# Two units' sums at once, a head in thirds, and four smaller moves in a hybrid scan, attention and STU kernel

## The chip, the cores and the metric

The kernel runs on one core of one Trainium2 chip. A core has a matrix engine (PE, with PEld for its weight loads), a vector engine (DVE), a scalar engine (ACT), GpSimd (POOL) and a queue that issues transfers (SP). Each works its own instructions in the order of the program; they meet through semaphores. The metric is the device time of one execution in microseconds (us), the median of several runs: 5449.74 us for the kernel before (three runs, 5448.53 to 5450.31).

## The reference

Four images of 48 x 48 positions and 128 channels, all in float32. Two layers follow each other:

```python
x = x + conv_ssm(gn(x))        # layer 0
t = tokens(x)                  # 2304 tokens of 128
t = t + attention(ln(t))       # softmax(q q^T) q, no projections
t = t + ffn(ln(t))             # spectral transform unit (STU)

# conv_ssm, cut: d = 256 inner channels, 16 states, K = 4 scan directions
xin, z = split(x @ in_proj)
xc = silu(depthwise_conv3x3(xin) + conv_b)
for each direction k:          # rows, columns, and both reversed
    dt = softplus(...);  B, C = projections of xc
    h = h * exp(dt * A) + dt * xc * B      # a recurrence over 2304 positions
    y_k = sum over the 16 states of h * C
y = layernorm(sum of y_k + D * xc) * silu(z) @ out_proj

# ffn, cut: 16 filters phi over the sequence, four sequence lengths mixed by weights
U_plus, U_minus = causal convolutions of u with each filter
out = sum_k U_plus @ M_plus[k] + U_minus @ M_minus[k] + three shifted products u @ M_u
```

## The kernel before

**Order of the work.** For each image b there is a prologue (norm, input projection, 3 x 3 convolution, silu), a scan pass, an epilogue with attention, and the STU. The prologue of image b + 1 runs inside the attention of image b, and the STU of image b inside the scan pass of image b + 1. So the program is: a head (prologue of image 0), pass 0, attention 0, pass 1 with STU 0, attention 1, pass 2 with STU 1, attention 2, pass 3 with STU 2, attention 3, and a last STU alone. The order is written out by hand with generators; the functions named below are all in one file.

**Head.** `prologue` makes a list of tasks. The convolution of one half of the channels (`taps`) is nine DVE operations over 128 x 2304 (L276, then L278 eight times); `silu` follows as a tanh on ACT (L287) and a product on DVE (L291) for each third of the half. `begin_scans` prepares the first chunks: projection xp (L412), dt (L429), softplus (L443), dx (L465), a store to DRAM and loads in the replicated form rep (L454, L459). It is a generator; in the head `begun` runs it through without anything between. `start_y` (L325) then starts the accumulators.

**Scan pass.** The 2304 positions in four directions are 24 chunks of 384. A chunk has eight units, (h, q): half of the channels, quarter of the states. A unit takes one step of the loop in `scans`: `enter` (L508, on DVE, or on POOL for three of the eight units) makes dt x B in a tile s, `decay` makes four decays on ACT (L517), `scan` runs four recurrences on DVE (L524), `times_c` multiplies by C (L534, POOL), and `sum_c` sums over the states by matmuls with a 128 x 32 matrix of ones (L542), four side by side on PE, into a y bank of the chunk. At step s the loop enters units s + 1 and s + 2, scans unit s, multiplies unit s - 1 and sums unit s - 2. There are six s tiles. The decays live in a `Ring` of PSUM banks (five in pass 0, four later), which also serves as space for the small products of `prep`; its constant zero columns are set once a pass (L341).

Between these, `more` takes the STU's work from a generator: it asks for the next piece while the columns done are fewer than the share of the pass that is over. `sum_c` adds its 384 columns to that count. The STU (`stu`) convolves with Toeplitz tables from DRAM: three products for each filter (L1192), copied by ACT between and after them (L1208, L1212, L1215, L1216), then projections (L1258). In pass 0 the generator is `mixture`, which mixes the weights.

**Attention.** Five pieces of up to 512 tokens, each in 18 slots. A slot is a score product (L852), an exp on ACT (L854) and, three slots later, a value product (L844). After a piece comes its `tail`, a generator that takes one step a slot: copy oT (L1043, DVE), transposes otr (L1047), denominators, the sum into T, a store td, and, for images that go on, a load tu, its statistics (L1072, then L1077 on POOL), the normed u (L1082, ACT), sums, transposes utr (L1088) and a store ud. The score products have three PSUM banks in turn.

**Last STU.** `stu3` works on three blocks of 128 rows by 16 filters. For each item it loads five tables (L1422) and a weight G (L1425), two items ahead; `begin` loads ux, mue and res for a block (L1431 to L1436). Five products (L1446) make x, y and i; DVE combines them into U (L1533 to L1537), and `project` multiplies by G (L1480) with U of the item before; the first time it also does the shifted products with mue (L1464). `finish3` prepares later blocks step by step beside it: a load fx (L1361), statistics (L1365), normed u (L1376).

What sets the order is thus the program order on each engine's queue. On SP all loads and stores stand in one line.

## Time and profile before

| | |
|---|---|
| median of three runs | 5449.74 us |
| profiled execution | 5450.86 us |
| its span, first to last instruction | 5448.9 us |
| PE busy | 4753.7 us (87%) |
| DVE busy | 4320.4 us (79%) |
| POOL busy | 3646.6 us (67%) |
| ACT busy | 3213.1 us (59%) |
| first to last scan of passes 0 to 3 | 117.8 to 1061.5, 1302.8 to 2258.4, 2497.5 to 3456.5, 3695.6 to 4651.1 |
| last STU, from its first product | 4847.0 |

The page gives busy times by engine, the span in 40 slices (a digit is tenths of busy time), the transfers, and groups of instructions by source line. Views of the trace used here are the timeline (start, length, engine, line, operation, and in brackets the idle time of that engine before it and what ended it), sums over windows, and lists of waits (who waited for whom: total, times, longest). PEclk is the granted share of PE's clock.

### The profile page before, as it was taken

To read this page: it belongs to the slowest core of one execution; us is meant where nothing else is said; L and a number is where in the kernel's file an instruction comes from. 1 tells how busy PE (TensorE), PEld (TensorE's weight loads), DVE (VectorE), ACT (ScalarE), POOL (GpSimd) and SP (SyncE) were. 2 spreads that over 40 slices of the span, in tenths; PEclk is the share of its full clock that TensorE was granted. 3 is DMA by queue.
4 is the path that set the end of the run, shared out by engine and by line. 5 is a ranking of instruction groups with operands and counts; after the bars stand their busy time and mean duration, and the time that the engine had idled before them with its cause. 6 is when DMAs were issued, how large, how long until landed. Compare 5 with 4: busy or idle time off the path is not lost. (4 is left out here: it accounts for less than half of the span.)

```text
span 5448.9 us, 71245 instructions
## 1 busy us (share of the span) xinstructions
PE 4753.7 (87%) x23372; PEld 3059.5 (56%) x23372; DVE 4320.4 (79%) x5308; ACT 3213.1 (59%) x6829; POOL 3646.6 (67%) x1881
## 2 busy tenths in 40 slices
PE   4656655698999999998999999898999999989999
PEld 1211211255666666645666666545666666559987
DVE  7999999856999999856999999658999999423211
ACT  3666666546777767456777766457777666432111
POOL 1999998713989999605999999407999999201100
PEclk7777777799999999999999999999999999999999
DMA  4445545404887777416777787227877786136543
GB/s 123 157 156 171 171 153 165 128 27 143 248 257 254 251 258 253 134 34 193 239 259 254 242 269 252 84 75 208 252 246 260 249 262 230 37 83 153 151 142 91
DMA packets 732184, 996.11 MB, mean 183 GB/s; under 512 B 108968, under 2 KB 580648, under 8 KB 731752
## 3 DMA queue, kind: packets, MB, share of 16 engines
q1 hardware_dynamic: 725992, 988.26, 57.6%
q10 hardware_dynamic: 5824, 3.30, 0.3%
q8 instruction: 187, 3.06, 0.2%
q14 instruction: 181, 1.48, 0.1%
HBM read 873.03 MB, written 118.31 MB: 182 GB/s over the span
## 5 line engine op out<-in xcount | busy, mean ns | idle before, releaser
L524 DVE TENSOR_TENSOR_SCAN s<-ring,s 128x385 f32<-128x385 f32 x3072 | 2691.5, 935 | 88.8 <-ACT ring L517 88.0
L534 POOL TENSOR_TENSOR s<-s,bc 128x1536 f32<-128x1536 f32 x763 | 2423.4, 3179 | 95.2 <-DVE s L524 39.0
L517 ACT ACTIVATE ring<-rep,A 128x384 f32<-128x384 f32 x3072 | 1760.2, 584 | 873.9 <-DVE s L508 537.2
L508 POOL TENSOR_TENSOR s<-rep,bc 128x1536 f32<-128x1536 f32 x288 | 994.7, 3454 | 152.4 <-DMA rep<-dtdud 81.2
L542 PE MATMUL y<-s,csum 128*32 128x384 f32 x6144 | 712.5, 538 | 184.0 <-POOL s L534 130.5
L508 DVE TENSOR_TENSOR s<-rep,ring 128x1536 f32<-128x1536 f32 x480 | 829.6, 1729 | 40.5 <-issue 19.9
L1192 PE MATMUL cx<-tt,u 128*128 128x252 f32 (+7 forms) x2880 | 621.9, 357 | 89.9 <-ACT cy L1208 88.9
L1192 PEld LDWEIGHTS cx<-tt,u 128*128 128x128 f32 x2880 | 501.7, 192 | 306.6 <-ACT cy L1208 135.4
L1192 PE MATMUL cx<-tt,us 128*128 128x252 f32 (+7 forms) x2880 | 617.3, 356 | 36.0 <-ACT U L1216 34.2
L1192 PEld LDWEIGHTS cx<-tt,us 128*128 128x128 f32 x2880 | 496.4, 193 | 196.7 <-issue 70.9
L1192 PE MATMUL cy<-tt,u 128*128 128x252 f32 (+5 forms) x2880 | 603.9, 351 | 0.0
L1192 PEld LDWEIGHTS cy<-tt,u 128*128 128x128 f32 x2880 | 490.7, 191 | 150.3 <-issue 99.4
L1258 PE MATMUL pr<-U,G 128*128 128x288 f32 (+4 forms) x1344 | 435.5, 451 | 6.8 <-DMA G<-gd 6.8
L1515 POOL TENSOR_TENSOR t<-s,s 128x512 f32<-128x512 f32 x48 | 63.4, 1320 | 521.7 <-ACT s L1513 521.7
L542 PEld LDWEIGHTS y<-s,csum 128*32 128x32 f32 x6144 | 126.0, 112 | 503.0 <-issue 237.8
L972 PE MATMUL G<-M,W 128*128 128x256 f32 (+3 forms) x512 | 242.3, 590 | 178.8 <-ACT Gm L948 81.2
L854 ACT ACTIVATE e<-s,shift 128x512 f32<-128x512 f32 (+1 forms) x360 | 230.7, 643 | 275.6 <-PE s L852 275.6
L852 PE MATMUL s<-xnT 128*128 128x512 f32 (+1 forms) x720 | 339.8, 557 | 12.9 <-ACT xnT L812 12.9
L844 PE MATMUL o<-e,xn 128*128 128x512 f32 (+1 forms) x720 | 335.4, 550 | 0.0
L1258 PEld LDWEIGHTS pr<-U,G 128*128 128x128 f32 x1344 | 232.4, 192 | 147.0 <-issue 89.2
L972 PEld LDWEIGHTS G<-M,W 128*128 128x128 f32 x512 | 106.9, 242 | 319.3 <-issue 111.3
L532 POOL COPY carry<-s 128x4 f32<-128x4 f32 x640 | 121.3, 189 | 230.8 <-DVE s L524 228.7
(236 smaller groups left out, 5029.5 us busy)
## 6 DMA issues: line engine op xcount, KB each, us to landing
rep<-dtdud SPq DMA_DIRECT2D x768, 384.0 KB
bc<-xdd SPq DMA_DIRECT2D x768, 192.0 KB
tt<-fd SPq DMA_DIRECT2D x144, 577.0 KB
tt<-fd SPq DMA_DIRECT2D x144, 451.0 KB
tt<-fd SPq DMA_DIRECT2D x144, 325.0 KB
dtdud<-dt SPq DMA_DIRECT2D x192, 192.0 KB
dtdud<-dx SPq DMA_DIRECT2D x192, 192.0 KB
t<-fd SPq DMA_DIRECT2D x80, 384.0 KB
```

The costliest lines, as they stand in the source:

```text
L508: eng.tensor_tensor(s, self.ch.rep[self.h][:, :, 1], bt.unsqueeze(1).to_broadcast([P, G4, CS]), ALU.mult)
L517: nc.scalar.activation(ring.body(self.dA[g]), ch.rep[self.h][:, g, 0], AF.Exp, scale=A[:, ch.k, self.h * G4 + g, self.q:self.q + 1])
L524: nc.vector.tensor_tensor_scan(s, ring.decays(i, ch.rev), s, 0.0, ALU.mult, ALU.add)
L532: nc.gpsimd.tensor_copy(carry[:, self.h, self.q].unsqueeze(2), self.s[:, :, end:end + 1])
L534: eng.tensor_tensor(self.s, self.s, ch.bc[Q4 + self.q].unsqueeze(1).to_broadcast([P, G4, CS]), ALU.mult)
L542: nc.tensor.matmul(ch.y[g * DL:(g + 1) * DL, :CS], csum, self.s[:, g], start=(self.q == 0), stop=(self.q == Q4 - 1))
L844: nc.tensor.matmul(po[J][:, :w], xn[:, i], e[:, :w], start=(i == 0), stop=(i == NT - 1))
L852: nc.tensor.matmul(p[:, :w], xnT[:, i * P:(i + 1) * P], xnT[:, 512 * J:512 * J + w], start=True, stop=True)
L854: nc.scalar.activation(e[:, :w], p[:, :w], AF.Exp, bias=shift)
L972: nc.tensor.matmul(p[:, :n], W[:, q if t else 0, i], M[t][:, i].unsqueeze(1).to_broadcast([P, n, C]), start=(t == 0 and i == 0), stop=(t = ...
L1192: nc.tensor.matmul(p4[:, 1:3, v - (hi - at):] if g else p4[:, 0:4:3, v - (hi - at):], x, t[:, :, hi - 1 - at + J * P:end if end >= 0 else ...
L1258: nc.tensor.matmul(o if q else o.rearrange("p f r m -> p r f m"), G, U[n][:, 4 * q:4 * q + 4, v0:v1].rearrange("p (a b) m -> p a b m", a=2 ...
```

## The change

Six places are edited.

1. **Head.** For image 0 the second half's convolution is done in thirds of 16 rows. The first third and its gate stay in the prologue; the operations of the other two thirds go into a list `late`, and the loop over `begin_scans` takes two of them after each of its first six pieces and one after each later piece. The prologue's pool moves to the other side of memory and is closed after that loop.
2. **Ring.** The zero columns are written by an ACT copy from the tile `none`, not by a DVE memset.
3. **STU ahead.** In passes 1 to 3 three steps of the STU are taken before the step loop begins.
4. **Sums.** `sum_c` is called at every second step, for units s - 3 and s - 2 together, and the count goes up by 768 there.
5. **Tail.** One more step between oT and otr; two more between the sums and utr.
6. **Last STU.** The five tables of the first item and the first mue are loaded in the last attention, 20 slots before its end, into a pool `pre` of their own; `fetch` leaves out the tables of item 0 and `begin` the first mue.

```diff
@@ -268,14 +268,14 @@
         def nothing():
             pass
 
-        def taps(h):
+        def taps(h, lo=0, hi=H):
             def tap(t):
                 dy, dx = divmod(t, 3)
-                x = xpad[:, dy:dy + H, dx:dx + W]
+                x, o = xpad[:, dy + lo:dy + hi, dx:dx + W], xc[h][:, lo:hi]
                 if t == 0:
-                    nc.vector.tensor_scalar(xc[h], x, cw[:, h, 0:1], cb[:, h:h + 1], ALU.mult, ALU.add)
+                    nc.vector.tensor_scalar(o, x, cw[:, h, 0:1], cb[:, h:h + 1], ALU.mult, ALU.add)
                 else:
-                    nc.vector.scalar_tensor_tensor(xc[h], x, cw[:, h, t:t + 1], xc[h], ALU.mult, ALU.add)
+                    nc.vector.scalar_tensor_tensor(o, x, cw[:, h, t:t + 1], o, ALU.mult, ALU.add)
             return [(nothing, Slow(lambda t=t: tap(t), 2.65), t == 0) for t in range(9)]
 
         def silu(h):
@@ -314,9 +314,18 @@
             if i % 2:
                 tasks.append(zs_[9 + i // 2])
                 tasks.append(silu(0)[i // 2])
-        tasks.extend(taps(1))
-        tasks.extend(silu(1))
+        if b:
+            tasks.extend(taps(1))
+            tasks.extend(silu(1))
+            return tasks
+        third, gates = H // 3, silu(1)
+        late[:] = [f for i in range(1, 3) for t in (*taps(1, i * third, (i + 1) * third), gates[i]) for f in t[:2]
+                   if f is not nothing]
+        tasks.extend(taps(1, 0, third))
+        tasks.append(gates[0])
         return tasks
+
+    late = []
 
     def start_y(b):
 
@@ -338,7 +347,7 @@
         def __init__(self, pool, n, name):
             self.t = [pool.tile([P, 512], F32, tag=f"ring{i}", name=f"{name}_{i}") for i in range(n)]
             for t in self.t:
-                nc.vector.memset(t[:, 0:CS + 2:CS + 1], 0.0)
+                nc.scalar.copy(t[:, 0:CS + 2:CS + 1], none[:, :2])
             self.free = list(range(n))
 
         def take(self):
@@ -666,6 +675,8 @@
         enter(-1)
         spread(1)
         fill(1)
+        for i in range(3 if units[0].ch.b else 0):
+            done[0] += next(work)
         for s in range(len(units) + 2):
             real = s < len(units)
             enter(s)
@@ -693,9 +704,10 @@
                 scan(s, 3)
             refill(s - 2, Q4)
             refill(s + 1, 0)
-            if s >= 2:
+            if s >= 2 and units[s - 2].q % 2:
+                units[s - 3].sum_c(back.psy)
                 units[s - 2].sum_c(back.psy)
-                done[0] += CS
+                done[0] += 2 * CS
                 if units[s - 2].q == Q4 - 1:
                     pending.append(units[s - 2])
             more((s + 1) / len(units))
@@ -1042,6 +1054,7 @@
         oT = pool.two.tile([P, 512], F32, tag="oT", name=f"oT{b}_{J}")
         nc.vector.tensor_copy(oT[:, :P * n], po[:, :P * n])
         yield
+        yield
         p = ps.trs.tile([P, 4, C], F32, tag="tr", name=f"otr{b}_{J}")[:, :n]
         for j in range(n):
             nc.tensor.transpose(p[:, j], oT[:, j * P:(j + 1) * P], ident)
@@ -1082,6 +1095,8 @@
             nc.scalar.activation(u[:k, J, j], x[:k, j], AF.Identity, bias=mv[:k, j, 3:4], scale=mv[:k, j, 2:3])
         yield
         nc.vector.tensor_tensor(sums[:k, J], u[:k, J, 0:2], u[:k, J, 2:4], ALU.add)
+        yield
+        yield
         yield
         p = ps.trs.tile([P, 512], F32, tag="tr", name=f"utr{b}_{J}")[:, :4 * k]
         for j in range(4):
@@ -1393,7 +1408,24 @@
             yield
         nc.sync.dma_start(ud3[:, :, 1 + P * G:1 + P * (G + 1)], x)
 
-    def stu3(b, pool, ps, u3, ue):
+    PT3 = (3, 1, 4, 0, 2)
+
+    def table3(pool, tag, k, pt, hi, name):
+
+        t = pool.tile([P, 2 * (L3 if tag == "tt" else P)], F32, tag=tag, name=name)[:, :2 * hi].rearrange(
+            "p (e i) -> p e i", e=2)
+        row = fd3[k, pt, 0]
+        nc.sync.dma_start(t, bass.AP(row.tensor, row.offset + L3 - hi, [[1, P], [L3 + P, 2], [1, hi]]))
+        return t
+
+    def mixed3(pool, bl):
+
+        parts = PARTS3[bl]
+        t = pool.tile([P, 3, 3, C], F32, tag="mue", name=f"mue3{bl}")
+        nc.sync.dma_start(t[:, :len(parts)], mud[:, parts[0][2]:parts[-1][2] + 1])
+        return t
+
+    def stu3(b, pool, ps, u3, ue, pre, ready):
 
 
 
@@ -1407,7 +1439,7 @@
         tts, Gs, S, U, now = {}, {}, {}, {}, {}
         last = pool.one.tile([P, KF], F32, tag="last", name="last3")
         nc.vector.memset(last, 0.0)
-        PT = (3, 1, 4, 0, 2)
+        tts.update({(0, pt): t for pt, t in zip(PT3, ready)})
         Y = 3 * (P + 1)
 
         def fetch(n):
@@ -1415,11 +1447,8 @@
                 return
             bl, k = items[n]
             hi = P * (bl + 1)
-            for pt in PT:
-                t = tts[n, pt] = pool.tt.tile([P, 2 * L3], F32, tag="tt", name=f"t3{n}_{pt}")[:, :2 * hi].rearrange(
-                    "p (e i) -> p e i", e=2)
-                row = fd3[k, pt, 0]
-                nc.sync.dma_start(t, bass.AP(row.tensor, row.offset + L3 - hi, [[1, P], [L3 + P, 2], [1, hi]]))
+            for pt in PT3 if n else ():
+                tts[n, pt] = table3(pool.tt, "tt", k, pt, hi, f"t3{n}_{pt}")
             parts = PARTS3[bl]
             Gs[n] = pool.tt3.tile([P, 2, 3, C], F32, tag="G", name=f"G3{n}")
             nc.sync.dma_start(Gs[n][:, :, :len(parts)], gd[k, :, :, parts[0][2]:parts[-1][2] + 1])
@@ -1430,8 +1459,7 @@
             now["x"] = pool.one.tile([P, 8, P], F32, tag="ux", name=f"ux3{bl}")
             nc.sync.dma_start(now["x"][:, 2:], ud3[:, :, 1 + lo:1 + hi])
             nc.sync.dma_start(now["x"][:, :2], ud3[:, 4:, lo:hi])
-            now["mu"] = pool.one.tile([P, 3, 3, C], F32, tag="mue", name=f"mue3{bl}")
-            nc.sync.dma_start(now["mu"][:, :len(parts)], mud[:, parts[0][2]:parts[-1][2] + 1])
+            now["mu"] = mixed3(pre.one, bl) if bl else ready[5]
             now["T", bl] = pool.two.tile([P, 6, C], F32, tag="res", name=f"res3{bl}")
             nc.sync.dma_start(now["T", bl], td[6 * lo:6 * hi].rearrange("(p j) c -> p j c", j=6))
 
@@ -1560,12 +1588,6 @@
         for _ in other:
             pass
 
-    def begun(pieces):
-
-        for x in pieces:
-            pass
-        return x
-
     def stu_alone(b, env):
         work = stu(b, env, 1)
         next(work)
@@ -1577,15 +1599,19 @@
         pool.close()
         tabs.close()
 
-    turn = Stage(tc, "p", "left", one=(1, SB))
+    turn = Stage(tc, "p", "right", one=(1, SB))
     begin0 = Stage(tc, "pp", "right", mm=(4, PSUM))
     once = Stage(tc, "once", "right", one=(1, SB))
     bank["mm"] = begin0.mm, ("t",)
     run(prologue(0, turn.one, mm_tile), 3, weights(once.one))
-    turn.close()
     once.close()
     front = Stage(tc, "f0", "left", one=(1, SB), xd=(2, SB), rep=(3, SB))
-    first = begun(begin_scans(0, front))
+    for i, first in enumerate(begin_scans(0, front)):
+        for f in range(2 if i < 6 else 1):
+            if late:
+                late.pop(0)()
+    assert not late
+    turn.close()
     begin0.close()
     start_y(0)
     for b in range(B):
@@ -1605,6 +1631,8 @@
         turn = Stage(tc, f"t{b}", "left", one=(1, SB))
         if b + 1 < B:
             tabs = Stage(tc, f"k{b}", "right", four=(4, SB))
+        else:
+            pre = Stage(tc, "pre", "right", one=(1, SB))
         back = Stage(tc, f"a{b}", "right", one=(1, SB), two=(2, SB), five=(5, SB))
         xn = back.one.tile([P, NT, C], F32, tag="xn", name=f"xn{b}")
         xnT = back.one.tile([P, L], F32, tag="xnT", name=f"xnT{b}")
@@ -1646,6 +1674,8 @@
             while parts and (spent < share * (i + 1) or i == slots - BEGIN - 1):
                 spent += costs.pop(0)
                 parts.pop(0)()
+        if not more:
+            ready = [table3(pre.one, f"t{pt}", 0, pt, P, f"t3{pt}") for pt in PT3] + [mixed3(pre.one, 0)]
         if more:
             turn.close()
             front = Stage(tc, f"f{b + 1}", "left", one=(1, SB), xd=(2, SB), rep=(3, SB))
@@ -1669,10 +1699,11 @@
     ps = Stage(tc, "endp", "right", psa=(1, PSUM), psc=(2, PSUM), psi=(1, PSUM), psp=(1, PSUM))
     bank["mm"] = ps.psa, ("mm",)
     ended = (x for G in range(1, N3) for x in finish3(G, extra, u3, ue))
-    for i, _ in enumerate(stu3(B - 1, pool, ps, u3, ue)):
+    for i, _ in enumerate(stu3(B - 1, pool, ps, u3, ue, pre, ready)):
         next(ended, None)
     ps.close()
     pool.close()
+    pre.close()
     extra.close()
```

## Prediction

> **What bounds the kernel now.** First the busy slices of the page.
>
> ```profile
> PE   4656655698999999998999999898999999989999
> DVE  7999999856999999856999999658999999423211
> PEclk7777777799999999999999999999999999999999
> ```
>
> Four scan passes (one an image) have DVE at 9; between them DVE falls to 5 or 6 and PE stays at 9 (attention); in the last seventh (the last STU) PE alone is full. The sums over windows of the four passes, then of the three stretches between them and the last:
>
> ```profile
> 117.80:1061.50 943.70, 558.49 (x2256) 184.59 (x2256) 908.42 (x932) 642.65 (x1377) 868.92 (x425) 0.74 0.48 157
> 1302.80:2258.40 955.60, 909.17 (x5037) 620.37 (x5037) 923.45 (x993) 683.34 (x1503) 872.32 (x424) 0.99 0.76 242
> ...
> 2258.44:2497.49 239.05, 217.68 (x762) 124.00 (x762) 118.51 (x257) 106.92 (x196) 23.92 (x33) 0.96 0.23 72
> ```
>
> The columns after the length are busy PE, weight loads, DVE, ACT, POOL. DVE is idle only 32 us of a pass's 956 (35 in pass 0): no edit inside a pass can bring more than that. Between passes PE is the bound. The waits of DVE in pass 1 (total, times, longest):
>
> ```profile
> DVE s L524 <- ACT ring L517: 24.7, 19, 3.7
> DVE s L508 <- POOL s L534: 2.1, 2, 1.5
> DVE ya L554 <- PE y L542: 2.0, 3, 1.0
> ```
>
> DVE waits for decays that ACT makes. Going through these waits one by one in the timeline: some 16 us are ten or so of the 4.2 us blocks in which ACT turns to softplus and back (two table loads of 1.28 us), at least 0.85 us of stall each; 7.9 us fall in the first chunk, and about 7 are moments where ACT stood before a copy that PE had not fed yet.
>
> **The change, part by part.**
>
> *Head by thirds.* Timeline of the head:
>
> ```profile
> 69.57 21.20 DVE L278 SCALAR_TENSOR_TENSOR xc<-xpad,cw,xc 128x2304 f32<-128x2304 f32 x8
> 92.75 4.21 PE L412 MATMUL xp<-xc,xw 128*128 128x384 f32 x6 [26.20 <-DVE xc L291]
> 102.78 1.03 DVE L465 TENSOR_TENSOR dx<-dt,xc 128x384 f32<-128x384 f32 x2 [8.21 <-ACT dt L443]
> 110.12 0.10 DVE L341 MEMSET ring<- 128x2 f32 x5
> 114.48 3.42 DVE L508 TENSOR_TENSOR s<-rep,ring 128x1536 f32<-128x1536 f32 x2 [4.27 <-issue]
> ```
>
> Nine taps over a half (68.06 to 90.8), then gates, then a chain xp, dt, softplus, dx, store, rep load (landed when POOL starts, 114.42), which lasts 21.7 us. Now nine taps over a third come first. A 768-element op of this kind took 0.95 us (L291), a third of 2.61 is 0.87; I take 0.95: 0.55 + 8 x 0.95 = 8.2, tanh 0.85 and gate 0.95 with hand-overs, so xp starts at about 78.3 instead of 92.75. The other two thirds follow among the pieces of begin_scans. The tanh of the second third waits on ACT until its taps end (78.3 + 8.2 = 86.5); behind it in ACT's queue stand the second dt copy, chunk 1's and the softplus: these resume at 87.4, and dx, behind three more taps on DVE, comes at 90.8 to 91.9 (before: to 103.8). By its old distance rep lands 10.6 later, 102.5. DVE: six taps to 97.7, tanh with one extra table load (1.28) to 100.0, gate, dx of chunk 1 and L325 (2.74): free at 104.8. So DVE, not rep, ends last: 114.48 - 104.8 = **9.7 saved** (5 to 13: DVE's idle 4.27 before L508 is what covers the smaller ops; without it the gain falls to 5).
>
> *Ring zeros from ACT.* The nearest row, the 128x4 copy of L515, took 0.19: four are 0.76 in a stretch where ACT sat 6.54 us before its first spread (waiting for DVE's memset behind the tail, 1298.81). The spreads, zero column and first exps queued behind them come before DVE is free, so DVE enters at 1298.81 instead of 1299.42: **0.6 x 3 = 1.8**; in pass 0 it is inside the 9.7.
>
> *Three STU steps ahead.* At the pass's start the copy that the next product needs (L1208) stands on ACT behind an exp that waits for DVE: PE sat 5.9 us, to 1303.80. Now that copy is issued before that exp; PE is some 3 us ahead. This bears on the first chunk's waits, 0.96 + 1.49 + 1.76 + 3.73; the last is mostly a softplus block. I take **1.5 x 3 = 4.5** (0 to 12). The three SP loads of L1223 to L1226 are issued a little sooner; SP has nothing urgent there.
>
> *y of two units.* Rows of PE in pass 1:
>
> ```profile
> 1800.34 0.85 PE L542 MATMUL y<-s,csum 128*32 128x384 f32 x8
> 1801.13 1.77 PE L1192 MATMUL cy<-tt,u 128*128 128x252 f32 x8
> 1802.73 0.81 PE L429 MATMUL ring<-xd,dtw 128*128 128x384 f32 x2
> 1803.38 2.09 PE L1192 MATMUL cx<-tt,us 128*128 128x252 f32 x10
> ```
>
> One unit holds PE 0.79 (1800.34 to 1801.13); the same columns in full-width form 0.65, and y also starts 0.09 late. A second unit right behind needs two passes of 0.35, so a pair saves about 0.19: 96 pairs, 18 us of PE a pass. The Trainium skill (TensorEngine Tiling (Array Packing), Tiling Modes) says that a change of tiling mode drains the engine; with the 398 cycles of fixed latency of a lone matmul at 2.4 GHz (TensorE: Matmul & The Clock Gate, Single matmul latency) a pair would save two drains, 0.33, or 32 us (an estimate from those pages). I go by the row. Either way PE is not the bound: it was idle or waiting for ACT there already. What it buys is ACT's waits for PE: of some 19 us a pass that hang on PE's lateness (7 in single waits, 7 above the floor of the softplus blocks, 4 to 5 in chunk 1) I give a sixth, 3 us. **3 x 3 = 9**, and 1 in pass 0, where PE has slack (558 of 944); by the skill's drain 5 us, 6 more in all. Bounds: -57 and +10. An s tile of an even unit is held a step longer; the reuse six allocations later still comes two steps after its sum, and the shortest distances (about 2.5 us) belong to tiles of odd units, whose sum moves back by only 0.7.
>
> *Tail steps.* PE's stalls in the stretch between passes 1 and 2, where PE bounds:
>
> ```profile
> 2370.23 1.65 ACT L1082 ACTIVATE u<-tu,umv 128x128 f32<-128x128 f32 x4 [5.72 <-POOL umv L1078]
> 2370.78 1.63 PE L1088 MATMUL utr<-ident,u 128*128 128x128 f32 x4 [4.62 <-ACT u L1082]
> 2385.07 0.44 PE L1047 MATMUL otr<-ident,oT 128*128 128x128 f32 x2 [1.41 <-DVE oT L1043]
> ```
>
> A slot is 0.87 us here and 1.72 with 512 columns; one more covers the 1.41. The 4.62 is not covered: u stands on ACT ahead of the exps, and it is u that waits (load, L1072, POOL). PE may run on one more slot, until its three score banks are full, then waits for the exp behind u. I take 0.6. **2.0 x 3 = 6** (-3 to 18). Eighteen calls still fit the eighteen slots of a piece; the last full tail loses two calls to after the loop, where ACT is free.
>
> *Last STU's tables sooner.*
>
> ```profile
> 4842.89 2.60 SPq L1422 DMA_DIRECT2D t<-fd  x5
> 4846.98 2.07 PE L1446 MATMUL x<-t,ue 128*128 128x256 f32 x4 [6.82 <-DMA t<-fd]
> 4860.43 0.33 SPq L1361 DMA_DIRECT2D fx<-td  x1
> 4867.81 1.26 DVE L1365 BATCH_NORM_STATS2 fs<-fx 128x6 f32<-128x128 f32 x6 [14.51 <-DMA fx<-td]
> 4871.16 4.10 PE L1480 MATMUL p<-U,G 128*128 128x144 f32 x16 [6.12 <-DVE U L1537]
> ```
>
> PE's first product can start at 4840.2, 6.8 sooner, but that is not what ends last: fx queues on SP behind 22 transfers, its statistics stand on DVE ahead of U, and PE waits for U. Six of the 22 (five tables, one mue) leave that queue: at (4867.8 - 4842.9)/23 = 1.08 us each, 6.5; by bytes (1.25 of 5.3 MB) 5.9. **6 saved.** The six are now issued some 35 us before attention's end, ahead of finish3(0)'s fx, which has 25 us to spare (4784.79 to 4809.94). A rule that speaks against more: the skill (TensorE: Matmul & The Clock Gate, Part 1) has PE at half clock after an idle window of about 3.4 us. The trace agrees: granted clock 0.53 in 4842 to 4853 and in 4870 to 4877; four matmuls took 2.07 and later 1.03. After the early products PE will wait about 7 us for U, so the project behind it starts at half clock again; at full clock it would bring 2.7 more (all its 30 matmuls took 6.27, the next 30 took 3.57). I count by the rule. Ends: 3, and 21 (all idle, both slow spells).
>
> **Sum:** 9.7 + 1.8 + 4.5 + 9 + 1 + 6 + 6 = 38.0. From the profiled execution, 5450.9 (span 5448.9 and 2.0 around it), that is 5412.9; it ran 1.1 above the median, so **5412 us**.
>
> **Rivals.** *PE's relief reaches DVE in full:* 19 us a pass instead of 4.5, 43 more: 5369; for half of that, 5390. For: nearly all ACT waits stand behind a PE copy. Against: softplus blocks come with a full ring too. *Only the ends count:* the edits in passes and tails move waits about; head, ring and tables leave 17.5: 5432. For: DVE is busy 97%. *It cancels:* as the last, and a new wait eats the rest: within 10 us of 5450. *Slower:* sixteen y matmuls hold PE 1.5 us in one go, ACT's copies of cx and U come later, the exps queued behind them empty the four-deep ring (a scan eats one each 0.86). The rest saves 28; the price that decides is 39/288 = 0.14 us of DVE a pair for 0.2%; at 0.25 a pair it is 5494. Against: ACT mostly is one or two exps ahead.
>
> **How the numbers follow.** Likeliest case 0.60 (own range 5400 to 5424), relief in half or more 0.15, ends only 0.16, cancels 0.04, slower 0.05. A change under 0.2% (10.9 us) can't be told from none here. Faster 0.91, same 0.04, slower 0.05. The range 5388 to 5435 takes in the first three but for the tail of the second.
>
> **What would show it.** L508's first DVE row at about 105; in passes 1 to 3 the first L508 right behind the tail's last DVE op; y rows of x16; PE's idle before utr near 4 and before otr gone; first L1446 row right after otr, fx about 6 sooner, U still waited for. Wrong if the passes' lengths move by more than 10 us each, if DVE waits for ACT ring grow above 25 us, or if attention's stretches lengthen.

## The result, and the profile after

The changed kernel took **5425.9 us** (5422.7 to 5427.2, five runs) beside 5449.5 (5447.1 to 5450.3) for the kernel before on the same chip: a ratio of 0.9959, 95% interval 0.9946 to 0.9972. That is 23.6 us, 0.4%, more than the 0.2% that can be told from no change. The forecast was 5412, range 5388 to 5435, with 38 us gained. Its profiled execution has a span of 5425.3, also 23.6 under the one before, so the two traces can be set against each other term by term. (Line numbers in the changed kernel are 9 to 28 higher: enter L517, spread L509, decay L526, scan L533, sum of y L551, copy or add of y L561 and L563, the last STU's products L1474 and L1508.)

First the page's 40 slices of the changed kernel; each digit is a busy share, or the granted clock, in tenths.

```profile
PE   4555555599999999998899999898899999989999
DVE  8999999856999999856999999658999999423211
PEclk7777777799999999999999999999999999999999
```

Nothing has changed hands: DVE fills the four passes, PE the attention and the last STU. The lengths of the stages of the changed kernel, as windows (length, then busy PE, weight loads, DVE, ACT, POOL, the granted clock, the share of the DMA engines and GB/s): pass 0, pass 1, and the stretch between passes 1 and 2 (from the last scan of the one to the first of the next).

```profile
111.92:1059.26 947.34, 523.06 (x2256) 198.03 (x2256) 909.06 (x932) 642.56 (x1377) 868.95 (x424) 0.73 0.47 155
1295.41:2250.80 955.39, 889.76 (x5034) 637.19 (x5034) 922.48 (x993) 681.88 (x1502) 872.65 (x426) 0.97 0.75 242
...
2250.80:2486.58 235.78, 219.07 (x770) 125.30 (x771) 118.46 (x254) 107.21 (x201) 26.69 (x33) 0.96 0.23 73
```

Pass 0 is 3.7 us *longer* than before (943.7). In pass 1 PE is busy 19.4 us less than before (889.8 for 909.2), as the pairs were to bring, though its granted clock fell from 0.99 to 0.97, and the pass is 0.3 shorter. The stretch is 3.3 shorter. By stages, from the two profiled executions:

| stage | before | after | difference | forecast |
|---|---|---|---|---|
| up to the first scan | 117.8 | 111.9 | -5.9 | -9.7 |
| pass 0 | 943.7 | 947.3 | +3.7 | -1 |
| passes 1, 2, 3 | 955.7, 959.0, 955.5 | 955.4, 955.6, 955.3 | -3.9 | -13.5 |
| stretches between passes | 241.3, 239.1, 239.1 | 236.2, 235.8, 235.7 | -11.8 | -7.8 |
| end of pass 3 to last otr | 189.0 | 188.4 | -0.6 | 0 |
| last otr to the end | 608.8 | 603.6 | -5.1 | -6 |
| sum | | | -23.6 | -38.0 |

So two places fell short, the passes by 14.3 us and the head by 3.8, and the stretches gave more than was asked. DVE's waits in pass 1 of the changed kernel (total, times, longest) show what became of the passes:

```profile
DVE s L533 <- ACT ring L526: 21.5, 18, 4.2
DVE ya L563 <- PE y L551: 8.6, 12, 1.9
DVE s L517 <- POOL s L543: 1.0, 1, 1.0
```

The wait for the ring fell from 24.7 to 21.5. The wait of the add for y rose from 2.0 to 8.6. The start of the pass did what was forecast of it: DVE's first enter comes at 1292.08, right behind its last operation on T, and where PE waited 5.92 us for ACT's copy, its longest wait is now 1.87.

The head, in the timeline of the changed kernel (start, length, instruction, idle time before it and who ended it):

```profile
79.37 3.69 PE L421 MATMUL xp<-xc,xw 128*128 128x384 f32 x6 [12.34 <-DVE xc L291]
92.82 1.02 DVE L474 TENSOR_TENSOR dx<-dt,xc 128x384 f32<-128x384 f32 x2
102.77 5.90 DVE L334 TENSOR_SCALAR ya<-xc,dsum 128x2304 f32<-128x2304 f32 x2
103.50 3.96 POOL L517 TENSOR_TENSOR s<-rep,bc 128x1536 f32<-128x1536 f32 x1 [70.91 <-DMA rep<-dtdud]
108.59 3.40 DVE L517 TENSOR_TENSOR s<-rep,ring 128x1536 f32<-128x1536 f32 x2
```

The chain came forward as forecast (xp at 79.4 for 78.3, rep landed at 103.5 for 102.5), but DVE's first enter did not come at 105: the two starts of y ahead of it took 5.90 us. Before the change the same two took 2.74.

The y rows of PE in pass 1, and PE's stalls in and after the attention between passes 1 and 2, changed kernel:

```profile
1790.54 1.50 PE L551 MATMUL y<-s,csum 128*32 128x384 f32 x16
1791.96 1.78 PE L1207 MATMUL cx<-tt,u 128*128 128x254 f32 x8
...
2360.93 0.91 PE L254 MATMUL ip<-xT,win 128*128 128x384 f32 x2 [0.87 <-DVE z L261]
2365.55 0.91 PE L864 MATMUL s<-xnT 128*128 128x256 f32 x2 [3.71 <-ACT e L866]
...
2377.88 0.38 PE L1060 MATMUL otr<-ident,oT 128*128 128x128 f32 x2
```

A pair holds PE 1.42 us (1790.54 to 1791.96), two singles held it 0.79 each. The 4.62 us stall before utr has become one of 3.71 before a score product, for the exp that stands behind u; new is 0.87 before it. Before otr at the middle of the stretch PE no longer waits (it was 1.41).

The last STU of the changed kernel, from the same timeline:

```profile
4821.48 1.03 PE L1474 MATMUL x<-t,ue 128*128 128x256 f32 x4
4829.29 1.13 PE L1474 MATMUL x<-t,ue 128*128 128x256 f32 x4 [3.33 <-DMA t<-fd]
4835.73 0.60 SPq L1376 DMA_DIRECT2D fx<-td  x1
4843.43 1.26 DVE L1380 BATCH_NORM_STATS2 fs<-fx 128x6 f32<-128x128 f32 x6 [16.28 <-DMA fx<-td]
4846.79 5.61 PE L1508 MATMUL p<-U,G 128*128 128x144 f32 x30 [6.93 <-DVE U L1565]
```

The first products run right behind otr at full speed; then PE waits for the second item's tables, and 6.93 us for U, which stands behind the statistics of fx on DVE, as forecast.

### The profile page after: what moved, and what is told of

It is laid out like the page before. It is cut to its first block, busy times and chain, and to the rows that moved or that the text cites. A ratio compares the mean times of both kernels' runs of the same rounds, so it can differ in the third digit from the quotient of the medians.

```text
span 5425.3 us, 71267 instructions
## 1 busy us (share of the span) xinstructions
PE 4658.1 (86%) x23372; PEld 3120.5 (58%) x23372; DVE 4324.9 (80%) x5309; ACT 3210.7 (59%) x6846; POOL 3656.8 (67%) x1881
## 5 line engine op out<-in xcount | busy, mean ns | idle before, releaser
L533 DVE TENSOR_TENSOR_SCAN s<-ring,s 128x385 f32<-128x385 f32 x3072 | 2691.4, 937 | 75.8 <-ACT ring L526 75.4
L526 ACT ACTIVATE ring<-rep,A 128x384 f32<-128x384 f32 x3072 | 1757.8, 584 | 885.5 <-DVE s L517 524.2
L517 POOL TENSOR_TENSOR s<-rep,bc 128x1536 f32<-128x1536 f32 x288 | 994.2, 3452 | 131.9 <-DMA rep<-dtdud 70.9
L517 DVE TENSOR_TENSOR s<-rep,ring 128x1536 f32<-128x1536 f32 x480 | 830.3, 1731 | 34.9 <-ACT ring L509 20.0
L551 PE MATMUL y<-s,csum 128*32 128x384 f32 x6144 | 646.9, 538 | 109.4 <-POOL s L543 88.9
L1207 PEld LDWEIGHTS cx<-tt,u 128*128 128x128 f32 x2880 | 514.9, 195 | 308.0 <-ACT cy L1223 181.3
L1207 PE MATMUL cx<-tt,us 128*128 128x252 f32 (+7 forms) x2880 | 597.6, 352 | 51.5 <-ACT U L1231 49.4
L1207 PE MATMUL cy<-tt,u 128*128 128x252 f32 (+5 forms) x2880 | 588.2, 349 | 0.0
L984 PE MATMUL G<-M,W 128*128 128x256 f32 (+3 forms) x512 | 222.7, 570 | 259.5 <-ACT W L974 134.7
L551 PEld LDWEIGHTS y<-s,csum 128*32 128x32 f32 x6144 | 166.3, 116 | 457.6 <-issue 259.0
```

Source lines behind the costliest of these rows:

```text
L517: eng.tensor_tensor(s, self.ch.rep[self.h][:, :, 1], bt.unsqueeze(1).to_broadcast([P, G4, CS]), ALU.mult)
L526: nc.scalar.activation(ring.body(self.dA[g]), ch.rep[self.h][:, g, 0], AF.Exp, scale=A[:, ch.k, self.h * G4 + g, self.q:self.q + 1])
L533: nc.vector.tensor_tensor_scan(s, ring.decays(i, ch.rev), s, 0.0, ALU.mult, ALU.add)
L551: nc.tensor.matmul(ch.y[g * DL:(g + 1) * DL, :CS], csum, self.s[:, g], start=(self.q == 0), stop=(self.q == Q4 - 1))
L984: nc.tensor.matmul(p[:, :n], W[:, q if t else 0, i], M[t][:, i].unsqueeze(1).to_broadcast([P, n, C]), start=(t == 0 and i == 0), stop=(t = ...
L1207: nc.tensor.matmul(p4[:, 1:3, v - (hi - at):] if g else p4[:, 0:4:3, v - (hi - at):], x, t[:, :, hi - 1 - at + J * P:end if end >= 0 else ...
```

## Experiments

Each kernel below is the changed kernel with the edits shown, unless it says "before with". This table has the stages of every profiled execution; the texts refer to it. "Enter" is the start of DVE's first enter. The runs were on several chips, where the kernel before took 5445.6 to 5447.8 us; each ratio is to before on the same chip.

| kernel | enter | pass 0 | passes 1 to 3 | stretches | otr to end | median of the runs |
|---|---|---|---|---|---|---|
| before | 114.5 | 943.7 | 955.7, 959.0, 955.5 | 241.3, 239.1, 239.1 | 608.8 | 5449.5 |
| after | 108.6 | 947.3 | 955.4, 955.6, 955.3 | 236.2, 235.8, 235.7 | 603.6 | 5425.9 |
| e1_single_sums | 108.4 | 943.7 | 954.8, 956.6, 955.3 | 239.1, 240.1, 237.4 | 601.6 | 5424.2 |
| e2_late_add | 107.8 | 937.4 | 953.7, 955.9, 956.0 | 237.4, 237.7, 238.6 | 599.9 | 5415.8 |
| e3_ya_act | 103.3 | 949.9 | 955.6, 955.7, 955.7 | 236.1, 238.9, 238.9 | 599.9 | 5426.9 |
| e4_fx_first | 108.9 | 946.8 | 955.8, 959.0, 955.6 | 239.3, 239.0, 235.8 | 596.3 | 5419.5 |
| e5_late_fx | 104.2 | 937.3 | 956.0, 956.8, 956.1 | 237.2, 235.4, 237.7 | 596.5 | 5413.1 |
| e6_late_fx_act | 104.2 | 939.4 | 955.9, 956.8, 956.1 | 236.5, 238.7, 237.8 | 596.1 | 5407.6 |
| e7_late_fx_act_single | 103.3 | 938.8 | 960.6, 962.2, 960.4 | 237.4, 240.9, 235.9 | 596.5 | 5428.2 |
| e8_only_tail | 115.0 | 944.1 | 960.5, 961.2, 959.5 | 236.6, 237.1, 240.5 | 610.8 | 5450.3 |
| e9_only_pairs | 112.9 | 947.5 | 956.5, 956.4, 956.4 | 238.5, 238.1, 238.3 | 609.7 | 5452.7 |
| e10_no_ahead | 104.7 | 945.9 | 959.4, 959.2, 955.7 | 236.1, 238.5, 238.9 | 600.2 | 5430.9 |
| e11_no_tail | 104.8 | 946.0 | 957.2, 957.1, 957.4 | 237.8, 237.4, 237.6 | 601.6 | 5434.2 |
| e12_all_three | 103.7 | 937.9 | 955.7, 955.6, 955.4 | 237.6, 235.8, 235.7 | 596.6 | 5411.6 |

A single profiled execution is one draw: with unchanged instructions a stretch came at 235.8 or 239.0 (e4), and the runs of before spread over some 20 us (5434 to 5458 on the chips of the later runs). Steps of under 2 us are therefore read from where in a stage they arise, and not from the totals. Part of this comes with the clock: the trace has spells in which PE is granted a clock of 0.5, called half clock below. The end varies too: with the same last STU it took 599.9 to 603.6 (after, e1, e2, e3, e10, e11). The head, the ring zeros and the tables had no run of their own; what is said of them are differences between these profiles.

### e1: single sums of y

```diff
-            if s >= 2 and units[s - 2].q % 2:
-                units[s - 3].sum_c(back.psy)
+            if s >= 2:
                 units[s - 2].sum_c(back.psy)
-                done[0] += 2 * CS
+                done[0] += CS
```

> The changed kernel with the sums of y taken one unit a step again; all else as changed. Theory A (the pair itself only moved a wait: y comes later on PE, so DVE's addition of y in passes 1 to 3, and ACT's copy of y in pass 0, wait for it): passes 1 to 3 stay within 2 us of 955.4, DVE's waits for y fall from 8.6 to about 2 us a pass while its waits for decays rise from 21.9 towards 25, pass 0 falls from 947.3 to about 943.5; total about 5422. Rival B (the pair brought the passes a gain, and another edit took it away): passes 1 to 3 grow by 3 us or more each, total 5430 or more. Rival C (the pair costs more than it brings): passes 1 to 3 shrink by 3 us or more each, total 5412 or less.

Measured: 5424.2 us, ratio to before 0.9960 (0.9947 to 0.9973), the same as with pairs. Pass 0 came back to 943.7, passes 1 to 3 stayed. DVE's waits in pass 1 here are the ring 23.8 us and the add 2.0, so what the pairs take from the one (2.3) they give to the other (6.6). The 17 to 19 us of PE that pairs save in each of passes 1 to 3 reached the span with nothing.

### e2: the add of y at the end of a step

```diff
-            if pending:
-                pending.pop().add_y()
             prepare(s)
...
             refill(s + 1, 0)
+            if pending:
+                pending.pop().add_y()
```

> The changed kernel with y added to its accumulator at the end of the step, after the fourth scan, and not after the second. Theory A (the wait for y is what ate the pair's gain): DVE's waits for y vanish, passes 1 to 3 fall by 5 to 7 us each, to about 949; in pass 0 ACT no longer stops for y, 947.3 falls to about 940; total about 5400. Rival B (DVE waits for decays in its place, since ACT and PE set the pace): waits for decays grow by what the others lose, passes 1 to 3 within 2 us of 955.4; total 5420 or more.

Measured: 5415.8 us, ratio 0.9944 (0.9926 to 0.9962). All of the 10 us lies in pass 0: 937.4. There the add is no DVE instruction but a PE product with the identity and an ACT copy of the sum, and ACT stands still in it. Timeline of the changed kernel in pass 0, at the longest of 17 such waits:

```profile
399.22 1.64 PE L554 MATMUL y<-ya,ident 128*128 128x384 f32 x2
400.89 0.82 ACT L561 COPY ya<-y 128x384 f32<-128x384 f32 x1 [4.42 <-PE y L554]
401.51 0.59 ACT L509 COPY ring<-bc 128x384 f32<-128x384 f32 x1
402.19 1.75 DVE L517 TENSOR_TENSOR s<-rep,ring 128x1536 f32<-128x1536 f32 x1 [3.78 <-ACT ring L509]
```

The copy waits 4.42 us for PE; the spread (L509) that DVE's next enter needs stands behind it on ACT, and DVE loses 3.78. In the whole of pass 0 the waits of ACT's copy and of DVE are, in the changed kernel

```profile
ACT ya L561 <- PE y L554: 32.4, 17, 4.4
...
DVE s L517 <- ACT ring L509: 18.6, 8, 3.8
```

and with the late add

```profile
ACT ya L561 <- PE y L554: 11.9, 9, 2.1
...
DVE s L517 <- ACT ring L509: 1.2, 2, 0.6
```

Before the change the first was 19.7: the pair added 12.7 us of it, since y's last sum now comes behind another unit's. DVE's idle time in pass 0 falls from 38.3 us to 8.7, and yet the pass is only 9.9 shorter. The rest went into the products dx, which DVE makes from two operands in SBUF (first the changed kernel, then this one: number, busy us, mean ns):

```profile
L474 DVE TENSOR_TENSOR dx<-dt,xc 128x384 f32<-128x384 f32 x44 | 54.9, 1286 | 0.0
L474 DVE TENSOR_TENSOR dx<-dt,xc 128x384 f32<-128x384 f32 x44 | 74.6, 1734 | 0.0
```

In these passes a dx takes 0.5 to 0.8 us where no product of POOL overlaps it, and up to 3.5 where one does; with the late add more of them overlap one (22 for 17, the head's included). Moving dx wasn't tried.

In passes 1 to 3 it was rival B that came true: the waits at the add went (0.2 to 1.3 us a pass), those for decays and spread rose from 22 to between 26 and 28, and the passes kept their lengths.

### e3: the first start of y on ACT

```diff
-    start_y(0)
...
         fill(1)
+        if b == 0:
+            yaccs[b] = [keep.tile([P, H, W], F32, tag=f"ya{h}", name=f"ya{b}_{h}") for h in range(NH)]
+            for h in range(NH):
+                nc.scalar.activation(yaccs[b][h], xcs[b][h], AF.Copy, scale=dsum[:, h:h + 1])
```

> The changed kernel with the accumulators of image 0 started by ACT, after the first decays, and not by DVE ahead of the scan. Theory A (the two DVE operations of 1.37 us took 5.90 because GpSimd's first product ran beside them): DVE's first product starts at 103.5 and not 108.6, total about 5 us less, 5421. Rival B (DVE would have waited for the loaded rows or the spread anyway): it starts at 107 or later, total within 2 us of 5426. Pass 0 itself may lose 1 us to ACT being busy 4 us longer.

Measured: the first enter came at 103.3, but the total did not move (5426.9, 0.9966, 0.9955 to 0.9977): pass 0 took 949.9, 2.5 more, and two stretches came at 238.9. The first half of theory A held. Of the 2.5 us, 2.3 arise in the first 32 scans.

### e4: fx issued first

```diff
     ended = (x for G in range(1, N3) for x in finish3(G, extra, u3, ue))
+    next(ended)
     for i, _ in enumerate(stu3(B - 1, pool, ps, u3, ue, pre, ready)):
```

> The changed kernel with the first load of finish3 issued ahead of the last STU's other loads. Theory A (U, and with it PE, waited only for the statistics behind this load): DVE's statistics no longer wait, PE's 6.9 us before the first project falls below 1, and the half clock after it goes: 7 to 9 us less, total about 5418. Rival B (the next tables are late as well): PE waits for tables or ux in its place, 3 us or less saved, total 5423 or more.

Measured: 5419.5 us, ratio 0.9955 (0.9940 to 0.9971). From the last otr to the end it took 596.3 instead of 603.6 (the profiled execution as a whole lies 10.6 over the median, with two stretches at 239). The end of e4, in its timeline:

```profile
4831.51 1.03 PE L1474 MATMUL x<-t,ue 128*128 128x256 f32 x4
4834.45 0.46 SPq L1376 DMA_DIRECT2D fx<-td  x1
4837.72 1.26 DVE L1380 BATCH_NORM_STATS2 fs<-fx 128x6 f32<-128x128 f32 x6 [0.41 <-DMA fx<-td]
4840.75 2.07 PE L1474 MATMUL x<-t,ue 128*128 128x256 f32 x4 [4.76 <-DMA t<-fd]
4851.14 3.60 PE L1508 MATMUL p<-U,G 128*128 128x144 f32 x30
```

The 6.93 us of waiting for U are gone, and the thirty projects behind it run at a granted clock of 1.00 instead of 0.64 and take 3.60 us instead of 5.61. Theory A holds, with a part of rival B: the second item's tables are now later, 4.76 us of waiting for 3.33. So it was fx, in its place on SP's queue, that ended last there. The 7.3 us are too much as a price, since the end of the changed kernel was the longest of its kind: against the other five with that last STU it is 3.6 to 5.3.

### e5: late add and fx first together

The edits of e2 and e4.

> The changed kernel with two edits together: y is added at the end of a scan step (as in e2_late_add), and fx is issued ahead of the last STU's own loads (as in e4_fx_first). Theory A, the two act in different stages and add up: pass 0 near 937.5 us instead of 947.3, from the last otr to the end near 597 instead of 603.6, passes 1 to 3 unchanged within 1 us (955 to 956), so 5425.9 - 9.9 - 6.6 = 5409. Rival B, the stretches between the passes decide more than the edits: their lengths go on taking values between 235.8 and 239.3 whatever the edit, so the total lies up to 5 us on either side of 5409 while pass 0 and the end are as A says.

Measured: 5413.1 us, ratio 0.9935 (0.9923 to 0.9948); pass 0 at 937.3 and the end at 596.5, so the two add up by stages; the median is 4 over the sum of theory A, inside rival B's 5. The profiled span is 5408.6, and it holds something that no edit made: the first enter came at 104.2, with the head's instructions those of the changed kernel. Its timeline there:

```profile
101.55 2.74 DVE L334 TENSOR_SCALAR ya<-xc,dsum 128x2304 f32<-128x2304 f32 x2
104.21 3.41 DVE L517 TENSOR_TENSOR s<-rep,ring 128x1536 f32<-128x1536 f32 x2
```

DVE's second start of y began at 102.88, POOL's first enter at 102.98, 0.1 us later; that enter then took 4.61 us. In the changed kernel, e1, e2 and e4 POOL began 0.2 to 0.7 us ahead of it, and the second start took 4.57 or 4.58 instead of 1.41.

### e6: with the first start of y on ACT as well

The edits of e2, e3 and e4.

> The kernel of e5_late_fx with the first y start on ACT as well (as in e3_ya_act). Theory A: e3 gave back 2.5 us in pass 0 because ACT's copies of y came later still and DVE waited for them at its add; with the add at the end of the step nothing waits there, so the 5.3 us of the start are kept: first scan near 106.6 instead of 111.9, pass 0 near 937.5, total some 5 us under e5_late_fx (5404). Rival B: what e3 gave back is ACT's time itself (two copies of 768 elements ahead of the decays of the first chunks, so that DVE waits for the ring): pass 0 near 940 to 943, total within 2.5 us of e5_late_fx.

Measured: 5407.6 us, ratio 0.9925 (0.9911 to 0.9938), the lowest median of all, though its interval and e5's overlap. Pass 0 took 939.4, and the 2.0 us over e5 all arise in its first 32 scans (+2.2 there, unchanged after). That is where rival B puts what e3 gave back, in ACT's own time for the two copies (of 2304 elements, not 768: 2.20 us each) among the first decays; the waits of ACT's copy of y, which theory A blamed, fell from 33.0 us in e3 to 11.7 here, and the loss stayed. The median, 5.5 under e5, is as theory A had it.

### e7: the same with single sums

The edits of e1, e2, e3 and e4.

> The kernel of e6_late_fx_act with y summed for one unit at a time again. Theory A, the pairs save only PE time that nothing waits for once the add is late: pass 0 within 2 us of e6, passes 1 to 3 within 1 us, total within 3 us of e6. Rival B, with the wait at the add gone the relief of PE does reach DVE (0.22 us a pair, 96 pairs a pass, half of it = 10 us a pass): without the pairs each pass is longer by 3 us or more and the total by more than 10 us.

Measured: 5428.2 us, ratio 0.9961 (0.9948 to 0.9973). Pass 0 does not care (938.8 for 939.4), but passes 1 to 3 are 960.6, 962.2 and 960.4, 4.3 to 5.4 longer than with pairs: neither theory in full, B's sign with half its size. PE's waits in pass 1 of this kernel say how:

```profile
PE cx L1210 <- ACT cy L1226: 19.1, 14, 4.7
PE y L551 <- DVE ya L563: 17.0, 16, 3.3
```

There is one y bank. With the add at the end of a step a single sum comes to that bank before DVE has emptied it and stands 17.0 us in this pass at the head of PE's queue; a pair comes a step later (3.3 us in e6). With the add in its old place singles wait there for nothing, and their passes are 954.8 to 956.6 (e1). Pairs are thus no gain over singles with the early add; they only let the add go late. A second y bank, which would test this directly, wasn't tried. In pass 0 the late add serves singles as well as pairs.

### e8: before with the tail steps alone

```diff
         nc.vector.tensor_copy(oT[:, :P * n], po[:, :P * n])
         yield
+        yield
...
         nc.vector.tensor_tensor(sums[:k, J], u[:k, J, 0:2], u[:k, J, 2:4], ALU.add)
         yield
+        yield
+        yield
```

> The kernel before with the three added tail steps alone. Theory A: PE's 1.41 us stall ahead of each otr goes, the 4.62 us stall ahead of utr turns into one of about 3.7 us for the exp behind u, so each of the three stretches between passes is 2 to 2.4 us shorter (239 near 237), the last attention 0.6 shorter; 5449.5 - 3 x 2.2 = 5443 by the sum. Rival B: the stretch lies at 235.8 or 239.1 by the pattern in which TensorE's clock is granted in it, and the edit only changes which pattern comes: single stretches jump by 3 us or not at all, and the passes, which the edit doesn't touch, stay within 1 us of 943.7 and 955.7.

Measured: 5450.3 us, ratio 1.0006 (0.9997 to 1.0014): no gain at all, though the stretches lost 5.2 us together. Passes 1 to 3, which neither theory moved, are 4.8, 2.2 and 4.0 longer, most of it in scans 33 to 64 (4.2 of the 4.8 in pass 1). There PE comes to a product whose weight G is still under way. The row in before, pass 1:

```profile
1375.04 0.75 PE L1258 MATMUL pr<-U,G 128*128 128x288 f32 x2 [2.01 <-DMA G<-gd]
```

and with the tail steps:

```profile
1372.39 1.32 PE L1261 MATMUL pr<-U,G 128*128 128x288 f32 x2 [2.48 <-DMA G<-gd]
```

The waits are nearly alike, but the product behind them takes 0.75 us in before and 1.32 here. The 7 us from that product on, in windows of before and of this kernel:

```profile
1375.04:1382.04 7.00, 6.94 (x42) 4.51 (x43) 5.84 (x8) 4.70 (x13) 6.84 (x5) 1.00 0.69 188
1372.40:1379.40 7.00, 7.00 (x25) 4.57 (x26) 4.08 (x5) 2.71 (x8) 6.84 (x5) 0.53 0.44 123
```

The granted clock is 1.00 in the one and 0.53 in the other, where PE gets through 25 matmuls instead of 42, and DVE is idle for 1.0 us around it in before and for 4.4 here. In before's own pass 2 the wait was 3.26, the clock behind it 0.76, and the pass 3.3 longer than its neighbours. G is issued on SP behind the rep loads of a chunk; that the shorter stretch brings PE there sooner and G not is the likely reason for the longer waits, and wasn't tested. Part of the profiled total is this execution's own, since it ran 9 us over the median of its kernel.

### e9: before with the pairs alone

The edit of e1 the other way round.

> The kernel before with the sums of y for two units at once alone. Theory A, the pair saves PE 0.22 us each but y comes later and the wait at its add takes what is saved: pass 0 near 947 (3.5 more than 943.7), passes 1 to 3 within 1.5 us of 955.5 with 6 to 7 us more of waits at the add and 3 less at the ring, total 5449.5 + 2 to 4 = 5452. Rival B, the prediction's term holds when the edit is made alone: passes 1 to 3 shorter by 3 us or more each, total 5441 or less.

Measured: 5452.7 us, ratio 1.0009 (1.0002 to 1.0016): 5.0 us slower than before, if anything. Two windows of this kernel, pass 0 and pass 1, and its waits at the add in pass 1:

```profile
116.28:1063.78 947.50, 514.92 (x2256) 195.78 (x2256) 910.16 (x932) 642.52 (x1377) 869.25 (x425) 0.74 0.48 157
1302.30:2258.82 956.52, 891.68 (x5040) 639.20 (x5041) 922.71 (x993) 682.34 (x1503) 872.15 (x425) 0.97 0.75 242
```

```profile
DVE s L524 <- ACT ring L517: 22.4, 19, 4.2
DVE ya L554 <- PE y L542: 8.6, 12, 1.9
```

Theory A: pass 0 is 3.8 longer, passes 1 and 3 are 0.8 and 0.9 longer, with PE 17.5 us less busy. (Pass 2 is 2.6 shorter, because before had its 3.3 us behind G there.) The 0.9 of pass 1 is a difference of larger parts: up to scan 384 the pass is 3.1 behind, and in the second half it wins back 2.3. So PE's relief may reach DVE in the second half; why not before, the runs don't show.

### e10: without the three STU steps ahead

```diff
-        for i in range(3 if units[0].ch.b else 0):
-            done[0] += next(work)
```

> The changed kernel without the three STU steps ahead of the first scan step. Theory A, they are what keeps the tail steps from costing in the passes (e8_only_tail lost 2.2 to 4.8 us in scans 32 to 64 of each pass, e1_single_sums, which has them, none): without them PE comes to pr with G not yet there for over 2.4 us, passes 1 to 3 near 958 to 960, total 5433 to 5439. Rival B, they are worth what the first 32 scans show (0.9 us a pass against before, ring zeros included): passes 1 to 3 within 1 us of 955.4, total 5426 to 5429.

Measured: 5430.9 us, ratio 0.9970 (0.9959 to 0.9981), 5 us over the changed kernel. The first 32 scans of passes 1 to 3 are 1.1 us longer each. By scan 192 passes 1 and 2 are 3.3 and 3.9 behind, pass 3 no more than 0.9. The wait for G is 0.7, 2.0 and 1.0 us here, so it can explain the second at most: the total lies between the two theories, and theory A's size came out in two passes of three, but not by its reason. The trace shows what goes with the rest. From scan 33 to scan 192 half clock was granted for 15.3 and 13.6 us in passes 1 and 2 (PEclk 0.96 and 0.97 there), and for 6.8 in pass 3 as in each pass of the changed kernel (PEclk 0.98). What brings it about in two passes and not in the third, with the same instructions, stays open.

### e11: without the tail steps

The edit of e8 the other way round.

> The changed kernel without the three tail steps. Theory A, they are worth 2 us in each stretch between passes: the stretches come to 238 to 239 instead of 235.8, PE's 1.41 us stall ahead of otr is back, the passes stay within 1 us, total 5426 + 6 to 8 = 5433. Rival B, e8_only_tail holds here too: what the stretches lose the passes gain (954 or less in passes 1 to 3), total within 2 us of 5426.

Measured: 5434.2 us, ratio 0.9983 (0.9975 to 0.9991), 8.3 over the changed kernel: theory A. PE's stall ahead of otr is back (1.51 us). The stretches are 237.8, 237.4 and 237.6, 1.6 to 1.9 longer at the same pattern of the granted clock. The passes, which were to stay, are 1.5 to 2.0 longer, by steps of about 1 us in scans 33 to 64 and, in passes 1 and 3, 129 to 192; why isn't known.

### e12: late add in pass 0 alone, fx first, y started before POOL begins

```diff
             if late:
+                if len(late) == 1:
+                    start_y(0, 0)
                 late.pop(0)()
+                if not late:
+                    start_y(0, 1)
...
-    start_y(0)
...
-            if pending:
+            if pending and units[0].ch.b:
                 pending.pop().add_y()
```

(with the second place of the add as in e2, `next(ended)` as in e4, and `start_y(b, h)` for one half)

> The kernel of e5_late_fx with two differences: y is added at the end of a step in pass 0 alone (where e2_late_add gained, and not in passes 1 to 3), and DVE starts y for the first half between the last tap and its gate, for the second right behind the gate, ahead of the dx of that third, so before POOL begins its first enter. Theory A, it is the order of the two at POOL's start that decides (POOL's first enter at 103.5 us, the second start of y before it in e5, e10 and e11: 1.41 us; behind it in the changed kernel, e1, e2 and e4: 4.57): both starts take 1.41 us here and DVE's first enter comes at 104.2 to 105.2 us in place of 108.6. Pass 0 near 937.4, passes 1 to 3 at 955.4, from the last otr to the end 596.5: the span is 5425.3 - 4 - 9.9 - 7 = 5404 with stretches of 235.8, and up to 9 us more with stretches up to 239. Rival B, DVE is held by POOL whatever the order (the starts of y or the dx behind them take 4 us or more): first enter near 108, span 5408 or more with stretches of 235.8.

Measured: 5411.6 us, ratio 0.9937 (0.9924 to 0.9951); profiled span 5405.6. Its head:

```profile
99.11 1.42 DVE L335 TENSOR_SCALAR ya<-xc,dsum 128x2304 f32<-128x2304 f32 x1
101.43 1.42 DVE L335 TENSOR_SCALAR ya<-xc,dsum 128x2304 f32<-128x2304 f32 x1
102.76 1.02 DVE L475 TENSOR_TENSOR dx<-dt,xc 128x384 f32<-128x384 f32 x2
103.70 3.41 DVE L518 TENSOR_TENSOR s<-rep,ring 128x1536 f32<-128x1536 f32 x2
```

POOL's first enter, 3.44 us, began at 103.70 as well. With both starts of y ahead of it each takes 1.42, and the first start also fills most of the 0.9 us in which DVE waited for the tanh. The enter comes 4.9 us sooner than in the changed kernel, for no work on ACT. Pass 0, passes 1 to 3 and the end are where theory A had them. Of e5, e6 and e12, all of them under both kernels, the runs can't tell which is best.

## Why the prediction was right or wrong

**Right in sign and inside its range, but 14 us too hopeful.** 5425.9 lies in 5388 to 5435, and 1.9 outside the likeliest case's own 5400 to 5424. By its mechanism the result stands nearest to the rival that only the ends count (5432): head, stretches, the way to the last otr and the end brought 23.4 of the 23.6 us. That it lies inside the range owes something to luck: the stretches gave 4.0 more than was asked while the pairs failed. None of the three signs of being wrong came.

**Pairs of y: the step that failed.** The saving on PE was about right: 0.19 a pair was read from the rows, and in the changed kernel a pair saves 0.16 of holding and the 0.09 of one late start; in pass 1 PE was 17.5 (e9) to 19.4 us less busy, where 18 was said. (The other estimate, 32 us, was not reached. Some of the saving may have gone into the clock, 0.97 for 0.99.) The wrong step is "of some 19 us a pass that hang on PE's lateness I give a sixth": it asked what PE's relief would bring ACT, and left out who waits for y itself. Alone the pairs cost 3.8 us in pass 0 and 0.9 in the others (e9), where 10 us of gain stood in the sum. In pass 0 the cause is shown: ACT's copy of y waits 32.4 us instead of 19.7, with the spread of the next unit behind it, and moving that copy brings 10 us (e2). In passes 1 to 3 y is late for the add on DVE, 8.6 us for 2.0, but that isn't the whole cause: with the add moved (e2) DVE waited for decays and spread instead. PE had more idle time, not less: it came sooner to the products that wait for ACT's cy (40.7 us in pass 1, 29.8 before). What keeps the relief from DVE there stays open. The rival "slower by bursts" had the direction for pairs alone, but not the place: the waits for the ring fell, and its price of 0.14 us a pair was not reached (3.8 us over 96 pairs are 0.04 in pass 0, and 0.01 in the others).

**Head by thirds: 9.7 said, 5.9 or 9.8 measured.** The forecast of DVE's first enter was 104.8; it came at 104.2, 104.7 and 104.8 in e5, e10 and e11, and at 107.8 to 108.9 in the changed kernel, e1, e2 and e4, with the same instructions. The mechanism and even the size hold; the term that failed is "L325 (2.74)", taken from a place where POOL was idle. A tap of a third took 1.05 us instead of 0.95, which over eight taps is most of the 1.1 us by which xp was late. (Before's own first enter came at 112.9 to 115.0 in three profiles, so the gain is known to a microsecond or two.)

**Ring zeros and steps ahead.** The stretches are 0.7 shorter with them (e11 against e9, like clock pattern), 2.1 in all where 1.8 was said. The three steps ahead give 1.1 us in the first 32 scans of a pass (e10) where 1.5 was said. Two passes of three gave 2 to 3 more, which wasn't foreseen; it goes with less half clock, and why is open.

**Tail steps: 2.0 a stretch said, 1.6 to 1.9 measured** (e11). The stall before utr became one behind the exp of u, 3.71 for "near 4", as argued. What was not in the sum: alone, the steps give it all back in the next pass, where PE meets G before its load and is then granted half clock (e8). In these runs the term is right only beside the steps ahead.

**Tables sooner: 6 said, 5.1 measured, and more in the other kernels.** U is still waited for 6.9 us, "about 7", at half clock again. But 603.6 is the longest of six ends with the same instructions, and two spells of half clock of 3.4 us in it, 53 and 592 us behind otr, are absent in e2, e3 and e10, which took 599.9 to 600.2. The means, 609.8 over before, e8 and e9 and 601.1 over the six, differ by about 8.7. So the term was nearer too small than too large. The reason given, fx in SP's queue, is shown by e4.

**The extra in the stretches is in part a draw.** They gave 11.8 us, where 7.8 was said. Before has 241.3, 239.1 and 239.1 and e9, with the same tail, 238.1 to 238.5, so 4.5 us lie between two profiles that differ in the pairs alone. In its first stretch before has 20.5 us of half clock and e9 17.3; the other two have the same pattern in both kernels and are still 0.8 to 0.9 longer in before, which isn't explained. The 3.3 us of before's pass 2 came with half clock behind the wait for G, as they did in pass 2 of e4. The profile of before held two rows that a second look would have doubted: one pass of three equal ones 3.3 longer, and one stretch 2.2 longer.

## What to carry to other kernels

When an engine's work is batched to save its time, the first question is who consumes the result and what stands behind that consumer in its queue; time saved on an engine that isn't the bound was worth nothing here, while moving the consumer of its result was worth 10 us in pass 0, and that pass is as short without the batching (e7). Count the idle time that such a move saves with care: two thirds of it went into instructions that then met a busy neighbour. Take a duration only from a place with the same neighbours: the price of two DVE instructions doubled because POOL worked beside them. And before a profile is used as the base of a sum, compare its repeated stages with one another, since the odd one out can be a draw of that execution and will seem to be a gain later; look at its granted clock first.

## What the runs showed of the hardware

**A DVE scale and a POOL product shut each other out.** The start of y, a 128x2304 multiplication by a per-partition scalar, took 1.41 us alone and 4.57 or 4.58 where POOL's enter had begun 0.2 to 0.7 us ahead of it; begun 0.04 to 0.15 us ahead of POOL it took 1.41 and POOL's enter 4.56 to 4.66 instead of 3.44. That is what the Trainium skill states (SBUF — State Buffer, Who interferes with whom): DVE's two-port modes, which such a scale can use, and GpSimd share a port pair, and whoever issues first has it for its whole instruction. The trace agrees in both orders, with 1.2 and 3.2 us as the price. A quarter of a microsecond of order (e10 and e2) decided 3 us of this kernel's time, and e12, which fixes the order, shows that it was the order. DVE's enter, with one operand in SBUF and one in PSUM, took 1.75 us beside a busy POOL (before, at 114.48) and 1.74 beside an idle one (the changed kernel, at 108.59), as the page has it for one SBUF input.

**The same attention stretch has more than one length.** In e10 the first stretch took 236.1 us and the second 238.5. The 35 us from 25 us into each, in windows of that kernel:

```profile
1079.00:1114.00 35.00, 30.15 (x174) 25.12 (x175) 22.30 (x97) 11.67 (x26) 10.08 (x17) 0.85 0.00 1
2274.44:2309.44 35.00, 30.77 (x170) 25.16 (x169) 21.64 (x93) 10.22 (x23) 9.13 (x14) 0.80 0.00 1
```

The clock is granted at 0.85 in the one and 0.80 in the other, and fewer matmuls get done (170 for 174): one block of 3.4 us more at half clock, 13.6 us for 10.2. The skill (TensorE: Matmul & The Clock Gate, Part 1) says that the gate looks at PE over windows of some 3.4 us that run free of the kernel; the blocks in the record are multiples of that, and that the same instructions fall on either side fits it. What fixes the phase in a given execution wasn't tried.

**What a late load costs depends on the clock behind it.** The wait of PE for one G, some 72 us into passes 1 to 3, was 0.2 to 3.3 us. Where the clock stayed whole behind it, a wait of 2.0 us cost DVE 1.0 (before) and one of 2.9 cost 2.0 (e7). Where half clock followed, waits of 2.0, 2.5 and 3.3 cost 2.8, 4.4 and 4.8 (e8). Of the 42 passes 1 to 3 in the fourteen profiles, eight had half clock right behind this wait (before's pass 2, e8's three, and pass 2 of e4, e5, e6 and e10); in these, scans 33 to 64 took 42.5 to 44.6 us, in the other 34 they took 39.6 to 42.2. The length of the wait doesn't decide alone which it is: half clock followed one of 1.9 us in e4 and not the one of 2.9 in e7. Issuing this G ahead of the rep loads wasn't tried.
